# Conv, causal attention and a mixture of experts on one core: when batch 0's last row sums and its results' gathers are issued

## The chip, the core and the metric

The kernel runs on one core of one Trainium2 chip. Its time is the device time of one execution in microseconds (us). The core has five engines that each work through their own list of instructions in order: PE (matrix products), DVE and ACT (elementwise work), POOL (elementwise work and indirect DMAs), and SP (which here only issues DMAs). The engines wait for each other through semaphores. PE reads its weights and its moving operand from SBUF and writes to PSUM; an output tile in PSUM is one "bank".

## The reference

Two images of 256 channels and 56 x 56 points go through a non-local convolution block, then, as 3136 tokens of 256 values each, through causal attention with four heads and through a mixture of eight experts of which each token uses its two best:

```python
# x: (2, 256, 56, 56)
x = conv_block(x)                      # groups of 1x1 convolutions, f = theta^T phi / n, y = f g, output 1x1, relu(. + x)
t = x.reshape(2, 256, 3136).transpose(0, 2, 1)
t = t + attention(layernorm(t))        # 4 heads of 64, causal, softmax, output projection
h = layernorm(t)
probs = softmax(h @ gate_w + gate_b)   # 8 experts
top2_vals, top2_idx = top_k(probs, 2)
for e in range(8):                     # only tokens that chose e have a weight
    y_e = gelu(h @ W1[e] + b1[e]) @ W2[e] + b2[e]     # 256 -> 512 -> 256
    t = t + weight_e[:, None] * y_e
out = t.transpose(0, 2, 1).reshape(2, 256, 56, 56)
```

## The kernel before, in words

**Attention** (`attend`, about L709 to L983). The queries are cut into rows of 448 (seven rows, `i`), the heads into two pairs (`hp`). For each row and pair the kernel goes over blocks of 128 keys: PE makes scores (L806), ACT their exponentials (L810), DVE adds these up in a tile `acc` (L829), and three steps later PE multiplies them with the values (L857) into a tile `yp`. There is one buffer of `yp` (two banks), so the first product of the next row and pair waits until ACT has copied the last one out (L867). POOL then adds the two halves of that copy (L868). The sums over the exponentials are made on PE by `sum_rows` (L878, four products with ones), copied by ACT (`store_sums`, L889) and sent to DRAM and back by SP, since the inverse is needed four steps later. If `sum_rows` was already issued for a row and pair, `acc` has been read, and L867 reuses it as its target (`both`); if not, `both` is a new buffer: from the pool of the scores' exponentials (tag "st", five buffers), or from that of `acc` at the very end. For rows `i > 0` the sums are issued before the values of the last blocks, for row 0 behind them. The visit called `final` belongs to the last row and pair of batch 1; its sums come behind everything.

**Experts** (`experts`, L1578 on). The (token, expert) pairs are sorted into blocks of 128 slots. A block's pass is one turn of the loop in `experts`: `hidden` (L1673, sixteen products), the transposes of the next input (L1650), `outputs` (L1692, eight products), with ACT's gelu (L1682) between, DVE's copy of a part of the next weights (L1661) and DVE's addition of the bias into a tile `ys` (L1702, two of them), of which there are three buffers. The first 42 blocks hold batch 0 only, the next 15 both batches, the rest batch 1. Blocks below 57 (`MIXED`) are stored as they are to the DRAM tensor `y_slots` by SP (L1707). Blocks from 42 on are scattered by POOL, with an indirect DMA, to the rows of `y_tokens` (L1713), where each token of batch 1 finds its two results. The last three blocks (99 and up) are kept in SBUF and placed by products with one-hot matrices (`place`, L1784) whose column numbers stand in three tiles `hots`.

**Bringing the results home** (`finish`, L1859 on). When block 56 has been put out, `written()` (L2277) opens the buffers for this and puts two generators into the queue, batch 1's ahead of batch 0's. Every turn, `meanwhile()` (L2286) sets the counters `gathered` and `stored` to 0 and asks the queue for four pieces. For batch 0 a piece is one gather by POOL (`fetch`, L1878: an indirect DMA of 128 rows of `y_slots`; 50 in all, four for each pair of token chunks), or a pair of adds by DVE (`add`, L1913: `res_f` and `y_f`), or a `store`: four transposes on PE (L1927, names `yo_f<-ident,res_f`), a copy by ACT into `ot` (L1932, two buffers for both batches together) and a store by SP (L1933). The condition at the head of the gather's loop sets how many gathers a turn may hold; `since` is the turn in which the generator starts. For batch 1 a piece is the load of `y_tokens` by SP (`load`, L1898), the adds (L1913, written into `y_f`) and the `store` (`yo_f<-ident,y_f`); they follow the blocks' progress and not the gathers. The last pairs of token chunks are treated by `last_rows`, `add_rows`, `place_rows` and `store_last` (L1744 to L1804). Three instructions of `number_columns` (L1854, an iota on POOL into `hots`) are issued between batch 0's gathers.

Instructions are issued on each engine in the order in which this program writes them; no scheduler moves them.

Of the kernel before, what the change touches and what calls it, by code (L numbers as in the profile page):

```python
# [10 lines left out]
F32 = mybir.dt.float32  # L11
# [17 lines left out]
def conv_attn_moe_kernel(  # L29
# [51 lines left out]
    nc = tc.nc  # L81
    P = 128
    B, C, N = x.shape
    NH = C // P
# [9 lines left out]
    NB = N // W  # L94
# [11 lines left out]
    OFF = 16 * N  # L106
# [4 lines left out]
    GB = 3  # L111
# [9 lines left out]
    LAST = max(n for n in range(NCH) if complete(n) <= DIRECT)  # L121
    REST = N - LAST * P
# [65 lines left out]
    with tc.tile_pool(name="c_w", bufs=1) as cw, tc.tile_pool(name="c_s", bufs=2) as cs, tc.tile_pool(  # L188
        name="c_big", bufs=5, space=PSUM
# [11 lines left out]
        for b in range(B):  # L201
            for col in (0, C + 1):
                nc.gpsimd.memset(xr[b][:, :, col : col + 1], 1.0)
            n = 0
# [54 lines left out]
        def channels():  # L259
# [12 lines left out]
            base=0, pattern=[[-D, G], [0, D]], channel_multiplier=1,  # L272
# [3 lines left out]
            base=D - 1, pattern=[[D, G], [0, D]], channel_multiplier=-1,  # L276
# [234 lines left out]
    def layer1(nm, general):  # L511

        with ExitStack() as whole:
# [195 lines left out]
            def attend(qT, kT, v, fst, fs, psc, py, open_batch, visit, between, clock, later, finished):  # L709

                steps = []
# [238 lines left out]
                for n in range(len(steps) + LAG):  # L950
                    copy_sums = None
                    if n in visits:
                        visit(*visits[n])
                        b, i, hp = visits[n]
                        if i == 0 and hp + 1 == NH:
                            turn_rows(b, 1)
                        if i > 0 and visits[n] != final:
                            copy_sums = sum_rows(b, hp, i)
                        aligned()
                    if n + 1 < len(steps) and n > LAG and steps[n][2] == 0 and steps[n - LAG - 1][2] == 0 and steps[n - LAG - 1][4]:  # L960
                        if steps[n][1] > 1:
                            turn_rows(*steps[n][:2])
                    if n < len(steps):
                        b, i = steps[n][:2]
                        if n == 0 or steps[n - 1][0] != b:
                            open_batch(b)
                        between(b, i, ends[b, i] - n, (steps[n][3] + 1) * P > i * W + 1, room(n))

                    late = n >= LAG and steps[n - LAG][4]
                    if n >= LAG:  # L970
                        due(clock[0])
                        clock[0] += 1
                    if n >= LAG and not late:
                        values(n - LAG)
                    if n in visits and visits[n][1] == 0:
                        copy_sums = sum_rows(b, hp, 0)
                    if copy_sums:
                        copy_sums()
                    if n < len(steps):
                        scores(n)  # L980
                    if late:
                        values(n - LAG)
# [866 lines left out]
                        ids.extend(experts_of(len(ids) // GB))  # L1849
                    between()  # L1850

            def number_columns(a):

                nc.gpsimd.iota(  # L1854
                    hots[a], pattern=[[1, REST]], base=LAST * P - OFF, channel_multiplier=0,
                    allow_small_or_imprecise_dtypes=True,
                )

            def finish(b, oy, bufs):  # L1859

                t = ts[b]
# [1 line left out]
                def fetch(n, m, k):  # L1863

                    ys = [
                        oy.tile([P, 2, C], F32, tag=f"y{b}{c}", bufs=bufs, name=f"y{c}_{nm}{b}_{n}")
                        for c in range(2)
                    ]
                    res = oy.tile([P, 2, C], F32, tag="res", bufs=bufs + 1, name=f"res_{nm}_{n}")
                    rows = res[:k, :m]  # L1870
                    nc.sync.dma_start(out=rows, in_=rest_d[:k, n : n + m])
                    ahead.append((n, m, k, ys, rows))
                    for c, y in enumerate(ys):
                        for a in range(m):
                            while gathered[0] == (1 if turn[0] < since + 4 else 2 - (turn[0] % 4 == 0)) or turn[0] < since + 2:
                                yield False
                            gathered[0] += 1
                            nc.gpsimd.indirect_dma_start(  # L1878
                                out=y[:k, a],
                                out_offset=None,  # L1880
                                in_=y_slots,
                                in_offset=bass.IndirectOffsetOnAxis(
                                    ap=idxs[b][:k, c, n + a : n + a + 1], axis=0
                                ),
                                bounds_check=MIXED * P - 1,
                                oob_is_err=False,
                            )
                            yield True
# [48 lines left out]

                ahead, added, since = deque(), None, turn[0]
                parts = deque(pairs())
                steps = deque(range(GB))  # L1940
                if b:
                    parts = deque([(0, 1, P), *pairs(1, LAST)])
                while b == 0 and (parts or ahead):
                    if parts:
                        yield from fetch(*parts.popleft())
                        if len(parts) % 2 == 0 and steps:
                            number_columns(steps.popleft())
                    if len(ahead) == bufs or not parts:
                        now = ahead.popleft()
                        yield from add(*now)  # L1950
                        if added:
                            while stored[0]:
                                yield False
                            store(*added)
                            yield True
                        added = now
# [296 lines left out]
            with ExitStack() as moe:  # L2253
                mw = pool(moe, "mw", bufs=1)
                ex = pool(moe, "ex", bufs=2)
                es = pool(moe, "es", bufs=3)
                ps6 = pool(moe, "ps6", space=PSUM)
                for k in range(len(w2s), KH):
                    t = mw.tile([P, E, C], F32, name=f"w2s{k}_{nm}")
                    w2s.append(t)  # L2260
                    for e in range(0, E, 2):
                        nc.sync.dma_start(
                            out=t[:, e : e + 2],
                            in_=w2[e : e + 2, k * P : (k + 1) * P].rearrange("e p d -> p e d"),
                        )
                for _ in load_w2(True):
                    pass
                while len(early_rows) < EARLY * GB:
                    pull(every=True)

                def need(b):
                    while not sent[b]:
                        pull(every=True)
                    while not ranked[b]:
                        next(side[0])

                def written():  # L2277
                    spread_rows.close()
                    oy = pool(moe, "oy", bufs=2, side="right")
                    last_pool.append(oy)  # L2280
                    hot = pool(moe, "hot", bufs=1, side="right")
                    hots.extend(hot.tile([P, REST], F32, name=f"hot{a}_{nm}") for a in range(GB))
                    queue.append(finish(0, oy, 2))
                    queue.appendleft(finish(1, oy, 3))

                def meanwhile():  # L2286
                    gathered[0] = stored[0] = 0
                    turn[0] += 1
                    if placed[1] and not sent[1]:
                        pull(1 + turn[0] % 2, every=True)  # L2290
                    else:
                        pull(
                            4 if worked[0] >= MIXED or projected[1] and not sent[1] or not chosen[0] else 2, every=True
                        )
                    if side and next(side[0], None) is None:
                        side.popleft()

                def amid():
                    if placed[1] and not sent[1]:
                        pull(every=True)  # L2300

                def settle():
                    while queue:
                        gathered[0] = stored[0] = 0
                        pull(every=True)

                def decide():
                    if not general:
                        assert judged
                        verdict.append(count(1))  # L2310

                with tc.manual_schedule(engines={PE, DVE, POOL, SP, ACT}):
                    experts(
                        first[0], w2s, b2s, ex, es, ps6,
                        meanwhile, amid, need, written, settle, decide,
                    )
# [172 lines left out]
```

## Time and profile before

| | us |
|---|---|
| median of three runs (lowest, highest) | 1267.23 (1265.88, 1269.42) |
| the profiled execution | 1266.76 |
| its span, first to last instruction | 1264.9 |
| L1673, the experts' first product: busy | 196.2 |
| L1713, 57 scatters on POOL: busy | 59.6 |
| L1661, 102 copies of weights on DVE: busy | 71.4 |
| DVE `res_f` L1913 waiting for a gather (2 times) | 1.1 |
| span's end after the last product's start (1257.41) | 7.5 |

The profile is of one execution. A row of its groups gives line, engine, operation, output and inputs by the program's names, shapes and count, then the busy time in us, the mean duration of one in ns, and the engine's idle time just before such instructions with what ended most of it. "issue" means that the engine waited for nothing that the profile shows. In the list of waits a line gives who waited for whom, the total in us, the number of times and the longest. A timeline row gives start and length in us, with the idle time before it in brackets. Ends of matmuls are modelled, so that neighbouring rows overlap a little.

The granted PE clock is full in all 40 slices of the span (mean 0.999). The chain of work that ended last runs over PE for nearly its whole length, with L1673 (14%), L1692 (13%), L806 (7%) and L857 (7%) the largest.

### The profile page before, as it was taken

How to read it: one execution, taken by the hardware profiler on the slowest of the kernel's cores; microseconds unless marked ns; L12 is line 12 of the kernel's file. 1: busy time of each engine (PE TensorE's matmuls, PEld its weight loads, DVE VectorE, ACT ScalarE, POOL GpSimd, SP SyncE). 2: the span in 40 equal slices, each digit the busy share in tenths (PEclk: the TensorE clock that was granted, in tenths of full speed). 3: DMA queues.
4: the chain of work that ended last, by engine and by line, in shares of the span. 5: the costliest groups of instructions: out<-in, count | busy, mean ns of one | idle time of the engine just before them, and what ended most of it. 6: DMA issues, size and time to landing. Idle time of an engine off the chain costs nothing.

```text
span 1264.9 us, 28755 instructions
## 1 busy us (share of the span) xinstructions
PE 1242.6 (98%) x10881; PEld 848.1 (67%) x10881; DVE 772.8 (61%) x1687; ACT 610.7 (48%) x1237; POOL 348.9 (28%) x318
## 2 busy tenths in 40 slices
PE   8999999999999999999999999999999999999997
PEld 8876655555454545655555444479889999988886
DVE  2582567666676574566677888785744443455563
ACT  0255555565656555465555656563334333343432
POOL 1103231110021103211111656000266012666650
PEclk9999999999999999999999999999999999999999
DMA  9996101000000000100000223641344433556653
GB/s 316 352 344 194 28 24 38 25 15 26 14 17 16 1 26 21 35 23 13 9 16 25 72 67 115 218 119 60 101 143 148 121 106 92 161 180 207 208 169 116
DMA packets 119875, 125.93 MB, mean 100 GB/s; under 512 B 28375, under 2 KB 109640, under 8 KB 119730
## 3 DMA queue, kind: packets, MB, share of 16 engines
q1 hardware_dynamic: 109074, 97.45, 25.3%
q0 software_dynamic: 9840, 25.67, 6.1%
q8 instruction: 90, 1.47, 0.5%
q10 hardware_dynamic: 816, 0.88, 0.2%
q14 instruction: 55, 0.45, 0.1%
HBM read 62.06 MB, written 61.05 MB: 97 GB/s over the span
## 4 chain that ended last, share of the span: by engine, by line
PE 47%; DVE 2%; issue 1%; ACT 0%; DVEq 0%
PE ht_f L1673 14%; PE yp_f L1692 13%; PE sc_f L806 7%; PE yp_f L857 7%; PE tp_f L1650 2%; PE pp_f L682 1%; PE yo_f L1927 1%; DVE y_f L1913 1%; PE qk_f L613 1%; PE v_f L628 0%; PE tail_f L1784 0%; DVE acc_f L829 0%; PE sp_f L878 0%; ACT st_f L810 0%; PE bp_f L1405 0%
## 5 line engine op out<-in xcount | busy, mean ns | idle before, releaser
L810 ACT ACTIVATE st_f<-sc_f 128x896 f32<-128x896 f32 (+5 forms) x400 | 331.2, 839 | 189.7 <-PE sc_f L806 164.4
L829 DVE TENSOR_TENSOR acc_f<-acc_f,st_f 128x896 f32<-128x896 f32 (+6 forms) x344 | 343.9, 1000 | 105.3 <-ACT st_f L810 93.2
L806 PE MATMUL sc_f<-qT_f,kT_f 64*64 64x448 f32 (+5 forms) x3136 | 345.3, 499 | 0.5 <-issue 0.3
L857 PE MATMUL yp_f<-st_f,v_f 64*64 64x448 f32 (+4 forms) x2896 | 323.5, 511 | 1.1 <-ACT acc_f L867 0.6
L806 PEld LDWEIGHTS sc_f<-qT_f,kT_f 64*64 64x64 f32 x3136 | 140.7, 133 | 133.6 <-issue 108.1
L1682 ACT ACTIVATE g_f<-ht_f,b1b 128x128 f32<-128x128 f32 x408 | 116.5, 371 | 226.1 <-PE ht_f L1673 111.4
L857 PEld LDWEIGHTS yp_f<-st_f,v_f 64*64 64x64 f32 x2896 | 122.5, 133 | 129.1 <-issue 105.0
L1673 PE MATMUL ht_f<-xT_f,w_f 128*128 128x128 f32 x1600 | 196.2, 275 | 4.0 <-issue 3.9
L1673 PEld LDWEIGHTS ht_f<-xT_f,w_f 128*128 128x128 f32 x1600 | 192.8, 192 | 8.8 <-issue 4.7
L1537 POOL DMA_INDIRECT x_slots<-xr_f,idx x100 | 113.6, 1136 | 148.4 <-DVE xr_f L1535 75.0
L868 POOL TENSOR_TENSOR qT_f<-acc_f 128x448 f32<-128x448 f32 x22 | 25.5, 1161 | 380.3 <-ACT acc_f L867 380.2
L1661 DVE COPY w_f<-w1s_f 128x1024 f32 x102 | 71.4, 701 | 86.0 <-PE ht_f L1673 38.6
L584 POOL TENSOR_SCALAR xn_f<-t 128x256 f32<-128x256 f32 (+1 forms) x50 | 80.3, 1613 | 130.0 <-DVE t L185 44.1
L1713 POOL DMA_INDIRECT y_tokens<-ys_f,to_f x57 | 59.6, 1046 | 126.4 <-DVE ys_f L1702 100.8
L1702 DVE TENSOR_TENSOR ys_f<-yp_f,kT_f 128x128 f32<-128x128 f32 x102 | 29.4, 289 | 96.6 <-PE yp_f L1692 63.6
L613 PE MATMUL qk_f<-px_f,wat 128*128 128x512 f32 (+2 forms) x224 | 87.2, 541 | 0.6 <-ACT px_f L605 0.6
L613 PEld LDWEIGHTS qk_f<-px_f,wat 128*128 128x128 f32 x224 | 40.6, 190 | 39.7 <-issue 33.7
L1692 PE MATMUL yp_f<-w2s_f,g_f 128*128 x204 | 60.9, 379 | 0.5 <-issue 0.5
L1692 PE MATMUL yp_f<-px_f,g_f 128*128 x204 | 61.1, 381 | 0.0
L1878 POOL DMA_INDIRECT y_f<-y_slots,idx x50 | 56.6, 1132 | 15.3 <-issue 15.3
L1692 PE MATMUL yp_f<-kT_f,g_f 128*128 x204 | 60.7, 379 | 0.0
L1692 PE MATMUL yp_f<-v_f,g_f 128*128 x204 | 60.7, 379 | 0.0
(299 smaller groups left out, 1308.0 us busy)
## 6 DMA issues: line engine op xcount, KB each, us to landing
x_slots<-fill SPq DMA_DIRECT2D x1, 8190.0 KB
xb_f<-x_slots SPq DMA_DIRECT2D x60, 130.0 KB
x_slots<-fill SPq DMA_DIRECT2D x1, 7296.0 KB
y_slots<-ys_f SPq DMA_DIRECT2D x57, 128.0 KB
kept<-t SPq DMA_DIRECT2D x2, 3200.0 KB
x<-in_x_dram SPq DMA_DIRECT2D x14, 448.0 KB
rb_f<-inverses SPq DMA_DIRECT2D x56, 112.0 KB
y_f<-y_tokens SPq DMA_DIRECT2D x23, 256.0 KB
```

The source lines that it names most:

```text
L584: nc.gpsimd.tensor_scalar(xn[:k, a], ts[b][:k, n + a, :C], ts[b][:k, n + a, MEAN : MEAN + 1], ts[b][:k, n + a, RSTD : RSTD + 1], ALU.subtr ...
L613: nc.tensor.matmul(ps[:, :w], wat[:, c, d0 : d0 + P], px[:, s % 2, c, :w], start=(c == 0), stop=(c == NH - 1),)
L806: nc.tensor.matmul(to, left, right, start=True, stop=True)
L810: nc.scalar.activation(st[rows, :, c0:], ps[rows, :, c0:W], AF.Exp, scale=SCALE)
L829: nc.vector.tensor_tensor(acc[rows, :, c0:], acc[rows, :, c0:], st[rows, :, c0:], ALU.add)
L857: nc.tensor.matmul(to, left, right, start=first, stop=end)
L1537: s = nc.gpsimd.indirect_dma_start(out=xds[b], out_offset=bass.IndirectOffsetOnAxis(ap=idxs[b][:kk, k, n : n + 1], axis=0), in_=xr[:kk], i ...
L1661: nc.vector.tensor_copy(w, w1s[:, :, bass.ds(e, 1), :].rearrange("p c e h -> p c (e h)"))
L1673: nc.tensor.matmul(ht[:, k, :], w[:, c, k * P : (k + 1) * P], xT[:, c, :], start=(c == 0), stop=(c == NH - 1),)
L1682: nc.scalar.activation(g[:, k, :], ht[:, k, :], AF.Gelu, bias=b1bs[b][:, k, i : i + 1])
L1692: nc.tensor.matmul(yp[:, :C], g[:, k, :], w2s[k][:, bass.ds(e, 1), :].rearrange("p e d -> p (e d)"), start=(k == 0), stop=(k == KH - 1),)
L1713: s = nc.gpsimd.indirect_dma_start(out=y_tokens, out_offset=bass.IndirectOffsetOnAxis(ap=to[:, n % GB : n % GB + 1], axis=0), in_=ys, in_o ...
```

## The change

Three edits.

1. In `attend`, the visit of batch 0's last row (`i == NB - 1`), second pair, is treated as those of row 0 are: its `sum_rows` is issued behind `values`. The same visit of batch 1 stays `final`.
2. The three iotas go from the gathers' loop into `written()`, one behind the other.
3. The gathers' loop waits under another condition. Before: none for two turns, then one a turn up to the fourth turn, then two, or one in every fourth turn. After: one a turn for eight turns, the first in the turn in which the generator starts, then one and two by turns.

```diff
-                        if i > 0 and visits[n] != final:
+                        short = i == 0 or (i, hp) == (NB - 1, NH - 1)
+                        if i >= 0 and not short:
                             copy_sums = sum_rows(b, hp, i)
                         aligned()
...
                     if n >= LAG and not late:
                         values(n - LAG)
-                    if n in visits and visits[n][1] == 0:
-                        copy_sums = sum_rows(b, hp, 0)
+                    if n in visits and short and visits[n] != final:
+                        b, i, hp = visits[n]
+                        copy_sums = sum_rows(b, hp, i)
                     if copy_sums:
                         copy_sums()
...
-            def number_columns(a):
-
-                nc.gpsimd.iota(
-                    hots[a], pattern=[[1, REST]], base=LAST * P - OFF, channel_multiplier=0,
-                    allow_small_or_imprecise_dtypes=True,
-                )
-
             def finish(b, oy, bufs):
...
-                            while gathered[0] == (1 if turn[0] < since + 4 else 2 - (turn[0] % 4 == 0)) or turn[0] < since + 2:
+                            while gathered[0] == (1 if turn[0] < since + 8 else 1 + turn[0] % 2):
                                 yield False
...
-                steps = deque(range(GB))
...
-                        if len(parts) % 2 == 0 and steps:
-                            number_columns(steps.popleft())
...
-                    hots.extend(hot.tile([P, REST], F32, name=f"hot{a}_{nm}") for a in range(GB))
+                    for a in range(GB):
+                        hots.append(hot.tile([P, REST], F32, name=f"hot{a}_{nm}"))
+                        nc.gpsimd.iota(
+                            hots[a], pattern=[[1, REST]], base=LAST * P - OFF, channel_multiplier=0,
+                            allow_small_or_imprecise_dtypes=True,
+                        )
```

The numbers of instructions on each engine are the same before and after; only their order differs. In that order the gathers of batch 0 stand like this against the scatters of blocks (S56 is block 56's scatter, G a gather, I an iota):

```
before: S57 S58G S59G S60GGI S61GG S62GG S63G S64GG S65GI S66GG S67G S68G S69GG S70GG S71I S72GG ... S89GG S90G S91G S92
after:  S56IIIG S57G ... S63G S64GG S65G S66G S67G S68GG S69G S70GG S71G S72G S73G S74GG ... S92GG S93G S94 S95GG S96
```

Batch 1's transposes stand where they stood. Batch 0's stand later: those of the pair at chunk 0 two turns later, at 12 three, at 20 and 22 four, and at 24 behind batch 1's at 17, in the last rows' part. On SP the stores of batch 0's pairs 20 and 22 thereby come behind the two loads (L1898) of batch 1's pair 19, which wait for the buffer of pair 17.

## The prediction

> **What bounds the kernel.** I read the engine table, then the waits over the whole run, then the timeline of the places the diff touches.
>
> ```profile
> PE 1242.6 (98%) x10881; PEld 848.1 (67%) x10881; DVE 772.8 (61%) x1687; ACT 610.7 (48%) x1237; POOL 348.9 (28%) x318
> ...
> L1702 DVE TENSOR_TENSOR ys_f<-yp_f,kT_f 128x128 f32<-128x128 f32 x102 | 29.4, 289 | 96.6 <-PE yp_f L1692 63.6
> ...
> L1878 POOL DMA_INDIRECT y_f<-y_slots,idx x50 | 56.6, 1132 | 15.3 <-issue 15.3
> ```
>
> PE is busy for 98% of the span of 1264.9 us: only what removes idle PE time, or shortens the start or the tail, can pay. No arithmetic is removed, so the prize is at most the idle PE time that the moved work causes. POOL is 28% busy, but its 50 gathers lie between 1082 and 1221, and there this average means nothing.
>
> **The gathers.** One expert block ("turn") is 16 matmuls of L1673, two of L1650 and eight of L1692. In the stretch before the gathers (990 to 1091) turns start exactly 3.73 us apart; a transpose of L1927 adds 0.11. From the end of one block's L1692 row at 1091.15 to another's at 1225.60 there are 32 turns and 75 transposes: 32 x 3.7325 + 75 x 0.11 = 127.7 us, but 134.45 passed. **6.8 us are lost here**, all in turns in which batch 1's transposes wait for DVE's adds (the profile's modelled waits give 4.2 us in 7 cases to L1927 <- DVE y_f L1913). The worst turn, PE first, then DVE, then POOL (start, length; idle in brackets):
>
> ```profile
> 1113.95 0.59 PE L1692 MATMUL yp_f<-w2s_f,g_f 128*128 x2
> 1115.70 0.33 PE L1927 MATMUL yo_f<-ident,y_f 128*128 128x128 f32 x1 [1.16 <-DVE y_f L1913]
> 1116.62 0.55 PE L1927 MATMUL yo_f<-ident,y_f 128*128 128x128 f32 x3 [0.59 <-DVE y_f L1913]
> ```
>
> ```profile
> 1109.92 0.85 DVE L1661 COPY w_f<-w1s_f 128x1024 f32 x1 [0.45 <-PE tp_f L1650]
> 1113.66 0.29 DVE L1702 TENSOR_TENSOR ys_f<-yp_f,kT_f 128x128 f32<-128x128 f32 x1 [2.89 <-PE tp_f L1650]
> 1113.87 0.28 DVE L1702 TENSOR_TENSOR ys_f<-yp_f,v_f 128x128 f32<-128x128 f32 x1
> 1114.64 0.48 DVE L1913 SCALAR_TENSOR_TENSOR y_f<-y_f,t 128x256 f32<-128x256 f32 x1 [0.50 <-issue]
> ```
>
> ```profile
> 1106.27 1.21 POOL L1713 DMA_INDIRECT y_tokens<-ys_f,to_f  x1 [2.16 <-DVE ys_f L1702]
> 1107.78 1.19 POOL L1878 DMA_INDIRECT y_f<-y_slots,idx  x1 [0.30 <-issue]
> 1109.28 1.00 POOL L1878 DMA_INDIRECT y_f<-y_slots,idx  x1 [0.30 <-issue]
> 1110.58 1.07 POOL L1713 DMA_INDIRECT y_tokens<-ys_f,to_f  x1 [0.30 <-issue]
> 1111.96 1.02 POOL L1878 DMA_INDIRECT y_f<-y_slots,idx  x1 [0.31 <-issue]
> ```
>
> The reader is to see that POOL runs without a rest, and that L1702, which before 1091 starts 0.20 us after its matmul has ended, starts here at 1113.66 for a matmul that ended at 1110.65: 3.0 late. The adds of L1913 stand behind it on DVE, and PE stops for them. A POOL DMA is about 1.0 us with 0.30 after it: two gathers and a scatter fill 3.9 us, more than a turn; one gather and a scatter fill 2.6. The late starts sort themselves by that: after two turns with two gathers each they are 1.7 to 3.0 us, after a single such turn mostly 0.2 to 0.7. Why a full POOL delays DVE, the trace does not say; that part is inference from a pattern.
>
> The old pace is one gather, then 2, 2, 2, 1 by turns, beginning two turns after block 56; the new one is one a turn for eight turns, beginning at once, then 1, 2, 1, 2. In the order of instructions no two turns in a row have two gathers any more; the first gather comes two turns earlier, the last some four turns later (behind the scatter of block 96 at the latest, in place of 92). So POOL needs 6.5 us in each two turns of 7.46. I expect the late starts to fall under about 1 us, which a batch 1 transpose bears (gaps appear from 1 to 2 us). Bounds: all 6.8 back, or nothing. **I take 5.4**, four fifths, since a turn with two gathers still meets some of batch 1's adds, and three times two adds of batch 0 (0.48 each) now follow batch 1's four in the same turn.
>
> Here a rule speaks against the change. The Trainium skill, "SBUF — State Buffer", in the box 'The "DVE blocks DMA" trap (SWDGE)', says that an fp32 SBUF-to-SBUF copy on DVE locks GpSimd out of the shared port while it writes a DMA's descriptors. Such a copy (L1661, 0.69 us) stands in every turn. Were that what fills POOL, spacing would not help, each gather would meet a copy anyway, and this part would bring nothing (sum: +0.85 us). The rows: gathers take 1.00 to 1.54 us, so a copy can cost one of them about 0.5, not the 2 to 3 us of the late starts; and two gathers a turn fill the turn even at 1.0. I go by the rows; the rule is part of why I don't take all 6.8.
>
> **The iotas.** Three of 0.52 us move from between gathers to before the first: 1.56 us on POOL after block 56's results. POOL was free there from 1074.4 to 1077.2, and no scatter waits. Cost 0. With the cover gone the first gather would be 1.5 us later, which a first add many turns on does not feel. The first gather waits for the last store to y_slots (issued by SP at 1073.2); at about 1076.3 that has landed if it takes 3 us, else POOL stalls for a fraction of a turn: cost 0 to 0.3 on POOL, taken 0 on PE.
>
> **The row sums.** In batch 0's last row, second pair, PE runs L878 (0.52 us), then the last values (L857), then waits 0.59 us at 475.69 for ACT to empty the one bank of yp:
>
> ```profile
> PE yp_f L857 <- ACT acc_f L867: 0.6, 1, 0.6
> ```
>
> With the sums behind the values ACT's copy starts 0.52 earlier, and the sums cover PE meanwhile: 0.5 to 0.59 us of gap go. Late next are PE's own matmuls. New: `both` takes one of the "st" buffers until POOL's add (L868, 1.13 us) is done, as every first row already does. If scores had to wait for that buffer, up to 0.5 would return. ACT's copy of the sums (0.35) and the loads behind it come up to 0.5 later, needed four steps on. **I take -0.55**; ends -0.6 and 0.
>
> **The tail, where something is added.** Batch 0's last stores slip: its transposes at 20 and 22 come three and four turns later, at 24 four (now directly behind batch 1's at 17). PE does the same number. But SP is a queue: the stores of 20 and 22 now stand behind the two loads of y19, which wait for a buffer that batch 1's transpose at 17 frees (they issue at 1250.75 and 1251.17). So store 20 issues at about 1251.65. `ot` has two buffers, in the order 20, 22, 17, 24, 19: the copy for 17 (L1932, 0.59) waits for store 20 to land, and the copy for 19, which ends the chain, waits for store 17 to land. With a landing time L after the issue, copy 19 can start at 1251.65 + 2L + 0.62 = 1252.27 + 2L; now it starts at 1258.05. The point from which this costs is L = 2.9 us. No row gives L for such a store in the middle. Nearest below: the second load of y19, issued 1251.17, used at 1254.31, so 3.1. Above: the last store, issued 1258.66, seen landed by SP at 1263.17, 4.5 with the last rows' stores ahead of it in the rings. Cost 0.4 to 3.3 us; nearer the lower, since store 17 flies alone but store 20 does not: L = 3.6, **+1.4 us**.
>
> **The sum.** -5.4 - 0.55 + 1.4 = -4.55 us. The profiled execution took 1266.76 us, of which 1264.9 is span: 1262.2, span 1260.35. The median of the three runs shown is 1267.23, 0.47 above that execution: **1262.7 us**. What this kernel's measurement can tell from no change is about 0.3%, 3.8 us; the forecast lies just beyond.
>
> **Rivals.**
> *The late starts stay.* They follow the number of gathers or the copy on DVE, not the density; the gaps only move to other turns. For it: 50 gathers before and after, more turns with gathers in them, and batch 1's transpose at 15 now close to their end. Against: turns with one gather show 0.2. Taking back 1.4 of the 6.8: 1267.23 - 0.55 - 1.4 + 1.4 = 1266.7.
>
> *The tail decides.* The two landings in series at the upper L = 4.5 cost 3.3. If the gathers' part gives nothing, the kernel is slower from L = 3.2 on (2L - 5.8 > 0.55); at 4.5 it is 1267.23 - 0.55 + 3.3 = 1270.0; if that part gives its 5.4, L would have to pass 5.9. For it: the queue order and buffers are fixed by the program. Against: no store's landing of such length is shown away from the crowded end.
>
> *The pacing does not take hold,* since pulls are shared with batch 1's work and gathers bunch anyway. The order of instructions shows them spread, so this has little: 1267 to 1268.
>
> **Chances.** Forecast 0.5 (own range 1260.0 to 1264.5: tail 0.4 to 3.3, gathers 4 to 6.8); late starts stay 0.27 (1264 to 1268.5); tail decides 0.17 (1267.5 to 1272); no hold 0.06. Leaving out a tenth at each side: 1259.5 to 1270.3. Faster by over 0.3% means under 1263.4: nearly all of the forecast's case, 0.47. Slower means over 1271: part of the tail's case and what I have not seen, 0.14. Within: 0.39.
>
> **What would show it.** Right: L1702's rows from 1080 to 1240 start under 1 us after their matmul, the wait L1927 <- DVE y_f L1913 falls from 4.2 to about 1, the wait of L857 for ACT at 475 is gone. Tail: ACT idles ahead of the copies for 17 and 19, and the time from the last L1927 to the last copy grows from 0.02 by about 1.4. Wrong: late starts of 2 us after turns with one gather; DVE rows waiting for gathers (now 1.1 us in two cases) or PE waiting for batch 0's adds, which would mean that the later results have become late themselves.

## The result, and the profile after

The changed kernel takes 1261.39 us (median of 7 runs, 1260.51 to 1263.36), the kernel before, beside it, 1267.23 (7 runs, 1265.34 to 1270.32): a ratio of 0.9958, 95% interval 0.9944 to 0.9972. That is 5.8 us, against the 4.6 forecast. The profiled execution has a span of 1259.3 us, 5.6 less than before.

The page's rows that answer to those shown of before:

```profile
PE 1241.6 (99%) x10881; PEld 849.1 (67%) x10881; DVE 775.7 (62%) x1687; ACT 611.0 (49%) x1237; POOL 348.8 (28%) x318
...
L1704 DVE TENSOR_TENSOR ys_f<-yp_f,kT_f 128x128 f32<-128x128 f32 x102 | 29.5, 289 | 89.3 <-PE yp_f L1694 66.3
...
L1873 POOL DMA_INDIRECT y_f<-y_slots,idx x50 | 56.1, 1123 | 17.1 <-issue 17.1
```

The same work, spread differently. The list of waits has lost L857 <- ACT acc_f (0.6 before), and of the 4.2 us for batch 1's adds this is left:

```profile
PE yo_f L1922 <- DVE y_f L1908: 0.9, 2, 0.4
```

To see where the time went, I set the two profiles beside each other matmul by matmul: the k-th product of a kind in one against the k-th in the other. The difference in start, after minus before:

```
where (time in before)          after - before, us
behind the start, 100 to 460        -0.98
after the row sums, 480             -1.50     the edit in attention: -0.52
760 to 880                          -2.30
routing done, 990                   -0.20     all of it given back
gathers begin, 1085                 -0.20
behind the gathers' stretch, 1235   -6.90     of which 1.3 are batch 0's transposes, moved behind it
last product, 1258                  -5.56
end of the span                     -5.6
```

So the whole gain lies between 1085 and 1258. The sum that gave 6.8 us of lost PE time before gives 1.5 us now. Batch 1's adds tell why. Seven groups of four lie in this stretch (the first group, of two, is left out); how late L1702 (L1704 after) starts just ahead of each:

```
group           2      3      4      5      6      7      8
before, us    3.01   0.20   2.65   2.53   2.43   2.13   2.41
after, us     0.89   1.06   0.20   1.87   1.08   0.20   1.46
```

Up to 1.08 PE does not wait; from 1.46 on it does. Over the whole stretch the late starts fell from a mean of 1.09 us to 0.78 and from at most 3.01 to 2.09, but starts more than 1 us late are hardly rarer: 15 of 34 turns before, 15 of 40 after.

The tail, in ACT's timeline of the changed kernel:

```profile
1248.99 0.94 ACT L1927 COPY ot_f<-yo_f 128x512 f32<-128x512 f32 x2 [6.77 <-DMA out_dram<-ot_f]
1251.30 0.53 ACT L1804 COPY hot_f<-tail_f 128x448 f32<-128x448 f32 x1 [1.38 <-PE tail_f L1786]
1251.87 0.40 ACTq L1805 DMA_DIRECT2D out_dram<-hot_f  x1
1253.49 0.58 ACT L1927 COPY ot_f<-yo_f 128x512 f32<-128x512 f32 x1 [1.66 <-DMA out_dram<-ot_f]
1254.11 0.38 ACTq L1928 DMA_DIRECT2D out_dram<-ot_f  x1
```

The first row is the copy for chunk 17 (with that for 24), which had to wait for store 20; the fourth is the copy for 19, which waits for store 17. Both waits stand where the prediction put them. Against PE's last product the last copy is 1.0 us later than before.

### The profile page after: what moved, and what is told of

Same layout as the page of the kernel before. It is cut to its first block, busy times and chain, and to the rows that moved or that the text cites. A ratio compares the mean times of both kernels' runs of the same rounds, so it can differ in the third digit from the quotient of the medians.

```text
span 1259.3 us, 28754 instructions
## 1 busy us (share of the span) xinstructions
PE 1241.6 (99%) x10881; PEld 849.1 (67%) x10881; DVE 775.7 (62%) x1687; ACT 611.0 (49%) x1237; POOL 348.8 (28%) x318
## 4 chain that ended last, share of the span: by engine, by line
PE 47%; DVE 1%; issue 1%; DMA 1%; ACT 0%; DVEq 0%; SPq 0%; ACTq 0%
PE ht_f L1675 14%; PE yp_f L1694 14%; PE yp_f L857 7%; PE sc_f L806 7%; PE tp_f L1652 2%; PE pp_f L682 1%; PE yo_f L1922 1%; PE qk_f L613 1%; DMA out_dram<-ot_f 1%; PE v_f L628 0%; DVE y_f L1908 0%; DVE acc_f L829 0%; PE sp_f L878 0%; PE bp_f L1407 0%; ACT st_f L810 0%
## 5 line engine op out<-in xcount | busy, mean ns | idle before, releaser
L857 PE MATMUL yp_f<-st_f,v_f 64*64 64x448 f32 (+4 forms) x2896 | 323.6, 511 | 0.5 <-DVE st_f L813 0.3
L857 PEld LDWEIGHTS yp_f<-st_f,v_f 64*64 64x64 f32 x2896 | 122.5, 133 | 128.2 <-issue 104.8
L1675 PE MATMUL ht_f<-xT_f,w_f 128*128 128x128 f32 x1600 | 197.4, 276 | 3.2 <-issue 3.2
L1675 PEld LDWEIGHTS ht_f<-xT_f,w_f 128*128 128x128 f32 x1600 | 193.4, 192 | 9.4 <-issue 5.0
L1704 DVE TENSOR_TENSOR ys_f<-yp_f,kT_f 128x128 f32<-128x128 f32 x102 | 29.5, 289 | 89.3 <-PE yp_f L1694 66.3
L1694 PE MATMUL yp_f<-w2s_f,g_f 128*128 x204 | 61.3, 381 | 0.2 <-issue 0.2
L1694 PE MATMUL yp_f<-kT_f,g_f 128*128 x204 | 61.1, 381 | 0.0
L1694 PE MATMUL yp_f<-v_f,g_f 128*128 x204 | 61.1, 381 | 0.0
L1694 PE MATMUL yp_f<-px_f,g_f 128*128 x204 | 61.1, 381 | 0.0
```

The lines of the kernel that those rows point to most:

```text
L857: nc.tensor.matmul(to, left, right, start=first, stop=end)
L1675: nc.tensor.matmul(ht[:, k, :], w[:, c, k * P : (k + 1) * P], xT[:, c, :], start=(c == 0), stop=(c == NH - 1),)
L1694: nc.tensor.matmul(yp[:, :C], g[:, k, :], w2s[k][:, bass.ds(e, 1), :].rearrange("p e d -> p (e d)"), start=(k == 0), stop=(k == KH - 1),)
```

## The experiments

The experiments ran on four chips (numbered 11, 1, 6 and 12), each with the kernel before beside it, and **on all four the kernel before takes 1250.4 to 1250.9 us, not 1267**. The chip of the result's own runs is not on record, nor is whether the chip or the hour made the difference. So what follows compares each kernel with the kernel before on its own chip; "the first place" is where and when the result was measured. Nothing but the two kernels of the result was measured there.

### The kernel before once more, and the three edits one at a time (chip 11)

> The kernel before, profiled once more, to see how far one execution differs from another. Theory (the change's gain lies in the gathers' stretch): PE's pace from 990 on is that of the first profile, with about 6.8 us lost between 1091 and 1226, while single differences of 0.5 to 2 us in the stretches before 990 (the load at the start, the routing between 885 and 986) come and go from execution to execution. Rival (those differences belong to the change): this profile agrees with the first one within 0.3 us everywhere before 990.

The program is instruction for instruction the same, and its span is 1248.2 us, 16.7 less. Matmul by matmul: 0.9 us at the start, 2.1 between 690 and 800 and 5.9 between 900 and 986 (in both stretches POOL scatters `x_slots`), nothing from 986 to 1090, 6.9 in the gathers' stretch, and 1.0 behind the last product. The theory fails where it seemed surest: between the gathers nothing is lost, and L1702 is 0.20 us late in all 34 turns with gathers. Here is a stretch with two gathers a turn, POOL, then DVE, then PE:

```profile
1096.85 1.02 POOL L1878 DMA_INDIRECT y_f<-y_slots,idx  x1 [0.30 <-issue]
1098.17 1.00 POOL L1878 DMA_INDIRECT y_f<-y_slots,idx  x1 [0.30 <-issue]
1099.48 1.02 POOL L1713 DMA_INDIRECT y_tokens<-ys_f,to_f  x1 [0.31 <-DVE res_f L1913]
1100.80 1.43 POOL L1878 DMA_INDIRECT y_f<-y_slots,idx  x1 [0.31 <-issue]
1102.24 0.52 POOL L1854 IOTA hot_f<- 128x448 f32 x1
1102.93 1.02 POOL L1713 DMA_INDIRECT y_tokens<-ys_f,to_f  x1 [0.17 <-issue]
```

```profile
1101.86 0.29 DVE L1702 TENSOR_TENSOR ys_f<-yp_f,kT_f 128x128 f32<-128x128 f32 x1 [0.52 <-PE yp_f L1692]
1102.06 0.28 DVE L1702 TENSOR_TENSOR ys_f<-yp_f,v_f 128x128 f32<-128x128 f32 x1
1102.84 0.55 DVE L1913 SCALAR_TENSOR_TENSOR y_f<-y_f,t 128x256 f32<-128x256 f32 x1 [0.50 <-issue]
```

```profile
1104.95 0.59 PE L1692 MATMUL yp_f<-w2s_f,g_f 128*128 x2
1105.38 0.60 PE L1927 MATMUL yo_f<-ident,y_f 128*128 128x128 f32 x4
```

This is the very turn that cost 2.2 us in the first place. POOL is as full, with the same iota between, and yet L1702 follows its matmul (end 1101.65) by 0.2 us, the adds end at 1104.83, and PE runs into batch 1's four transposes at 1105.38 without a stop. A full POOL is not enough to make the late starts.

> Only the row sums of batch 0's last row, second pair, go behind the values. Theory: the gap of 0.59 us at 475 goes, and PE runs 0.5 us ahead from there; but the routing stage between 885 and 986 swallows it, because it waits for a chain that is not PE's, so that from 990 on PE stands where it stood before: total 0 to -0.5 us (1266.7 to 1267.2). Rival: the 0.5 us reaches the end, and part of the change's 5.6 us is due to it: -0.5 us or more.

```diff
-                        if i > 0 and visits[n] != final:
+                        short = i == 0 or (i, hp) == (NB - 1, NH - 1)
+                        if i >= 0 and not short:
                             copy_sums = sum_rows(b, hp, i)
...
-                    if n in visits and visits[n][1] == 0:
-                        copy_sums = sum_rows(b, hp, 0)
+                    if n in visits and short and visits[n] != final:
+                        b, i, hp = visits[n]
+                        copy_sums = sum_rows(b, hp, i)
```

1250.91 us against 1250.74: ratio 1.0002 (0.9993 to 1.0010). PE gains 0.52 us at 475, loses 0.19 of it near 780, and the rest at the routing, where this line appears that the kernel before does not have:

```profile
PE rank_f L1291 <- DVE both_f L1243: 0.5, 1, 0.5
```

PE arrives 0.5 us early for a product whose operand a chain on DVE makes, and waits. The changed kernel shows the same line in both places. The theory holds: the edit pays 0.5 us and nothing of it reaches the end.

> Only the condition of the gathers' loop is changed; iotas and row sums stay. Theory: nearly all of the change's gain, -5 to -6 us (1261 to 1262): between 1091 and 1226 PE loses 1.5 us in place of 6.8, and the copy of chunk 19 waits about 1 us for a store. Rival (the iotas between the gathers matter): -3 us or less, with late starts of 2 to 3 us where an iota stands between two gathers.

```diff
-while gathered[0] == (1 if turn[0] < since + 4 else 2 - (turn[0] % 4 == 0)) or turn[0] < since + 2:
+while gathered[0] == (1 if turn[0] < since + 8 else 1 + turn[0] % 2):
```

1251.11 us: ratio 1.0003 (0.9995 to 1.0011). Neither theory is met: where the kernel before has no late starts, there is nothing to gain. What remains is the tail: the copy for 17 waits 6.9 us for a store and that for 19 another 2.0. In its profile the span is 1.8 us longer than in the one just shown; 0.7 of that stand from the start of the kernel on, 1.1 come behind PE's last product.

> Only the three iotas go to the front of the gathers. Theory: nothing that can be measured, 0 +- 0.5 us, as 1.56 us of 57 us of POOL's work go from the crowded stretch: the late starts of L1702 stay at 1.7 to 3.0 us. Rival (the iotas fill POOL just where it overflows): -1 to -3 us, with the worst turn at 1110 gone.

The edit is the change's second part alone (the iotas in `written()`). 1250.58 us, ratio 1.0000 (0.9992 to 1.0008): no effect, as expected, though without the late starts it can't be told what they would do in the first place.

### The changed kernel elsewhere, and its tail (chip 1)

> The changed kernel itself once more, beside the kernel before on the same chip. In the four runs before this one the kernel before took 1250.7 us and L1702 was never late between the gathers, where the first profile had 1.7 to 3.0 us. Theory A (the late starts are a condition of where it runs, and the change only treats them): where the kernel before shows no late starts (about 1250), the change is worth -0.5 to +1 us; where it shows them (about 1267), -5 to -6 us. Theory B (the change is worth 5 us anywhere, by its three edits together): -5 us here too.

1251.39 against 1250.72 us: ratio 1.0005 (0.9997 to 1.0013). Theory A: the change is worth 5.8 us in one place and nothing in another (it is 0.7 us slower, within the noise). ACT's last copies, chunk 17 with 24 and then 19:

```profile
1239.79 0.94 ACT L1927 COPY ot_f<-yo_f 128x512 f32<-128x512 f32 x2 [6.96 <-DMA out_dram<-ot_f]
...
1244.57 0.59 ACT L1927 COPY ot_f<-yo_f 128x512 f32<-128x512 f32 x1 [2.13 <-DMA out_dram<-hot_f]
```

> The changed kernel with three buffers for the tile that the copies of L1927 fill, in place of two. Theory (two landings in series hold up the last copy by 1.0 us in the profile after, 2.0 with the pacing alone): the copy of chunk 17 waits no longer for the store of 20, nor 19's for that of 17; ACT's waits for a store fall from 8.4 us to 0; the end comes 0.5 to 2 us earlier than in the changed kernel. Rival (the wait costs nothing, since the last store then has the DMA engines to itself): same time within 0.3 us.

```diff
-                    ot = oy.tile([P, NH, 2 * P], F32, tag="ot", bufs=2, name=f"ot_{nm}{b}_{n}")
+                    ot = oy.tile([P, NH, 2 * P], F32, tag="ot", bufs=3, name=f"ot_{nm}{b}_{n}")
```

The copies for 17 and 19 no longer wait for a store (that for 24 still does, 3.6 us), and copy 19 starts 1.44 us earlier:

```profile
1235.42 0.59 ACT L1927 COPY ot_f<-yo_f 128x512 f32<-128x512 f32 x1 [2.57 <-issue]
...
1243.13 0.59 ACT L1927 COPY ot_f<-yo_f 128x512 f32<-128x512 f32 x1 [0.66 <-PE yo_f L1922]
```

but the kernel takes 1251.32 us, the same as with two buffers: in time the rival is right. In its profile the last store was issued at 1243.75 and its last packets moved at 1248.07, 4.3 us later; with two buffers it was issued at 1245.19 and done at 1247.53, 2.3 us later. The other last stores had moved by 1245.6 in both. What the copy waits less, its store takes longer. Why is not shown: its last packets moved 2.5 us behind those of the other stores.

### More gathers a turn (chip 1)

> The kernel before with three gathers in every turn instead of one or two, and room in the queue's turn for them (12 pieces in place of 4). Three gathers and a scatter fill 5.2 us of POOL, more than a turn's 3.73, for all 17 turns. Theory A (a full POOL delays what DVE and ACT see of PE, anywhere): late starts of L1702 of 1 to 3 us in most of these turns also where the kernel before shows none, PE loses 5 us or more, time +3 to +8 us. Theory B (a full POOL alone does nothing; the late starts are a condition of where it runs): where the kernel before takes about 1250, L1702 keeps its 0.20 us save where its own buffer is not free; time within 1 us of before, or lower, as the stores come earlier.

```diff
-while gathered[0] == (1 if turn[0] < since + 4 else 2 - (turn[0] % 4 == 0)) or turn[0] < since + 2:
+while gathered[0] == 3 or turn[0] < since + 2:
...
-                            4 if worked[0] >= MIXED or projected[1] and not sent[1] or not chosen[0] else 2, every=True
+                            12 if worked[0] >= MIXED or projected[1] and not sent[1] or not chosen[0] else 2, every=True
```

1287.7 us, ratio 1.0294 (1.0276 to 1.0311), far beyond either theory, and in its time not a clean test. The 12 pieces also act on an earlier stage: 13 us are lost before the first gather. And in the gathers' stretch the adds now come right behind their gathers, so that DVE, in order, stops for the landing:

```profile
DVE res_f L1913 <- DMA y_f<-y_slots,idx: 35.7, 21, 5.0
```

(1.1 us in two cases in the first profile). It shows what the queue's small piece count is worth: the distance between a gather and its add hides the landing. DVE's late starts here, up to 6.8 us and in 10 of the 17 turns, can't be told from such waits.

ACT can be read, though, since its gelus (L1682) don't stand behind those waits. In the first place it saw PE late as DVE did. I count the gelus ahead of which ACT stood idle, and how late each begins after the last product of L1673 ahead of it. In the kernel before 13 of 27 in the gathers' stretch are more than 0.4 us late, at most 3.8, and 13 of 19 between 900 and 990, but none of 25 between these stretches, where the most is 0.20. In the changed kernel it was 13 of 29 and 12 of 18. Here POOL issues for 92 us without a rest:

```profile
1140.05 1.00 POOL L1878 DMA_INDIRECT y_f<-y_slots,idx  x1 [0.30 <-issue]
1141.36 0.99 POOL L1878 DMA_INDIRECT y_f<-y_slots,idx  x1 [0.30 <-issue]
1142.66 1.02 POOL L1713 DMA_INDIRECT y_tokens<-ys_f,to_f  x1 [0.30 <-issue]
1143.99 1.42 POOL L1878 DMA_INDIRECT y_f<-y_slots,idx  x1 [0.31 <-issue]
1145.71 1.00 POOL L1878 DMA_INDIRECT y_f<-y_slots,idx  x1 [0.30 <-issue]
```

and all 16 such gelus are at most 0.35 us late. So on this chip a POOL as dense as in the worst turn, and for 92 us on end, does not make ACT see PE late.

### Stores from another queue; POOL busy without DMAs (chip 6)

> The changed kernel with the stores of batch 0's pairs 18, 20, 22 and 24 issued from ACT's queue, right behind their copies, so that they don't stand behind the loads of y19 on SP. Theory (the tail's cost is SP's order; more buffers did not help because the stores themselves were still late): ACT's waits for a store (7.0 and 2.1 us in the changed kernel) go, the stores of 20 and 22 land 5 us earlier, the last 3 us have the DMA engines to themselves; 0.5 to 1.5 us less than the changed kernel, so at about 1250 no more than the kernel before. Rival (ACT, in order, is held by 0.4 us for each issue and delays gelus): no gain or a loss of up to 1 us.

```diff
-                            store(*added)
+                            store(*added, nc.scalar if added[0] >= LAST - 5 else nc.sync)
                             yield True
...
-                    store(*added)
+                    store(*added, nc.scalar)
                     return
```

ACT no longer waits for a store, and the last product (1242.08 us) and the last store's last packet (1245.45) stand where they stand in the kernel before (1242.01 and 1245.43, in the profile of chip 11). Yet it takes 1252.53 us against 1250.44: ratio 1.0017 (1.0009 to 1.0025), 2.1 us slower than the kernel before, where the changed kernel was 0.7 slower on chip 1. The expectation fails, and so does its rival, behind the work: SP, in its closing waits, stands still from 1246.13 to 1248.14, when the data has long moved. Why is open; in the one profile there is one more 8 KB fetch of instructions in the tail than in that profile of the kernel before, the last at 1248.78.

> Only the pacing, once more, on the chance of a place where the kernel before takes about 1267. There: the theory that the pacing carries the change's gain expects -5 to -6 us; the rival (iotas or row sums carry it) at most -3. Where the kernel before takes about 1250: +0.4 us as in the first run.

1251.55 us against 1250.44: ratio 1.0008 (1.0001 to 1.0014). Again there are no late starts to remove, and here the small loss, 1.1 us, is just clear of the noise.

> The kernel before with each of the 50 gathers replaced by four iotas on POOL into the same tile (batch 0's tokens are given numbers in place of their experts' results): POOL is as busy, but issues no DMA. Where the kernel before takes about 1267: if a busy POOL makes the late starts, they stay at 1.7 to 3.0 us and PE loses 6 us; if it is the gathers' DMAs, they are gone and PE loses nothing. Where it takes about 1250 there are none in either case, and the run shows only that.

```diff
-                            nc.gpsimd.indirect_dma_start(
-                                out=y[:k, a],
-                                out_offset=None,
-                                in_=y_slots,
...
+                            for _ in range(4):
+                                nc.gpsimd.iota(
+                                    y[:k, a], pattern=[[1, C]], base=0, channel_multiplier=0,
+                                    allow_small_or_imprecise_dtypes=True,
+                                )
```

```profile
1095.39 0.99 POOL L1713 DMA_INDIRECT y_tokens<-ys_f,to_f  x1 [0.43 <-DVE ys_f L1702]
1096.39 2.01 POOL L1879 IOTA y_f<- 128x256 f32 x4
1098.83 1.08 POOL L1713 DMA_INDIRECT y_tokens<-ys_f,to_f  x1 [0.43 <-DVE ys_f L1702]
1099.92 3.61 POOL L1879 IOTA y_f<- 128x256 f32 x8
1103.96 1.22 POOL L1713 DMA_INDIRECT y_tokens<-ys_f,to_f  x1 [0.43 <-DVE y_f L1908]
```

This kernel leaves the gathers out, so that batch 0's output is wrong, and has a single run, 1252.12 us. POOL is fuller than with gathers (four iotas take 2.0 us), scatters slip by up to 4 us, and L1702 is 0.20 to 0.38 late in 32 of 34 turns; in one of the others its row names the wait, a scatter that still holds its buffer. So where there are no late starts, neither a POOL full of iotas nor, in the run with three gathers a turn, a POOL full of DMAs makes them. The half of the question that needs the first place was not answered.

### The start alone, and the rule about DVE's copies (chip 12)

> The kernel before with its old densities (one gather, then 2, 2, 2, 1), but beginning two turns earlier; iotas and row sums stay. Where the kernel before takes about 1267: if spacing the gathers is what pays, this brings nothing (within 1 us); if their start is, -4 us or more. Where it takes about 1250: the stores of batch 0 come two turns earlier than before, so the tail stays as it was and the time is that of the kernel before within 0.5 us, against +0.4 to +1.1 us with the new pacing.

```diff
-while gathered[0] == (1 if turn[0] < since + 4 else 2 - (turn[0] % 4 == 0)) or turn[0] < since + 2:
+while gathered[0] == (1 if turn[0] < since + 2 else 2 - (turn[0] % 4 == 0)):
```

1250.4 against 1250.6 us: ratio 0.9998 (0.9989 to 1.0007). The tail stays as it was; no copy waits for a store. Of the new paces tried it is the only one that shows no cost there, and it is not measurably better than the kernel before.

> The kernel before with the copy of the weights (L1661, fp32 from SBUF to SBUF, 0.69 us on DVE) put on ACT for blocks 57 to 98, so that no DVE copy meets a gather. Where the kernel before takes about 1267: if the copy's hold on a port shared with POOL makes the late starts, they go and the time falls by 5 us or more; if not, they stay. Where it takes about 1250 there is nothing to gain: gathers take 1.00 to 1.10 us each in place of up to 1.5, ACT has about 1.1 us more a turn and stays under 3.73, time within 1 us of before, or a few us more if ACT's order delays the gelus.

```diff
-                    engines=(PE, DVE),
+                    engines=(PE, DVE, ACT),
...
-                    nc.vector.tensor_copy(
+                    copy = nc.scalar.copy if MIXED <= n < DIRECT else nc.vector.tensor_copy
+                    copy(
                         w, w1s[:, :, bass.ds(e, 1), :].rearrange("p c e h -> p c (e h)")
```

1250.68 us, ratio 0.9998 (0.9989 to 1.0007). The gathers' rows, first with the copy on DVE (chip 11), then with it on ACT:

```profile
L1878 POOL DMA_INDIRECT y_f<-y_slots,idx x50 | 55.7, 1115 | 15.3 <-issue 15.0 <-PE tp_f L1650 0.3
```

```profile
L1879 POOL DMA_INDIRECT y_f<-y_slots,idx x50 | 51.6, 1032 | 15.3 <-issue 14.7 <-PE tp_f L1650 0.3 <-DMA xb_f<-x_slots 0.3
```

Ten of the 50 gathers took over 1.3 us (at most 1.48) beside the copies on DVE; none does without (at most 1.21). The median stays 1.02. The rule of the Trainium skill that the prediction weighed, "SBUF — State Buffer", 'The "DVE blocks DMA" trap (SWDGE)', is seen here, in the size that the prediction read from the rows: up to half a microsecond for a gather that meets a copy, 4 us of POOL in all, and nothing of the time. Whether it has a part in the first place's late starts was not tested there.

## Why the prediction was right, and how far

**The gathers: right in size, in its place, and in part by luck.** -5.4 was taken, and 6.8 - 1.5 = 5.3 is what the aligned profiles give. The mechanism holds as far as this: shorter delays reach batch 1's adds, and up to 1.08 us PE does not feel them. But three statements of that step are wrong.

First, the late starts were to fall under about 1 us; they fell to at most 2.1, and as many turns as before have more than 1. Even the prediction's own sign of being wrong, 2 us after turns with one gather each, is there, at block 60:

```profile
1087.22 2.15 PE L1675 MATMUL ht_f<-xT_f,w_f 128*128 128x128 f32 x16
1088.66 0.69 DVE L1663 COPY w_f<-w1s_f 128x1024 f32 x1 [3.45 <-PE yp_f L1694]
1088.66 1.14 ACT L1684 ACTIVATE g_f<-ht_f,b1b 128x128 f32<-128x128 f32 x4 [5.28 <-PE yp_f L1694]
1089.27 0.28 DVE L1704 TENSOR_TENSOR ys_f<-yp_f,kT_f 128x128 f32<-128x128 f32 x1
```

(The product of L1694 had ended when L1675 starts, at 1087.22.)

Second, what paid is which turns are hit, and this the forecast did not work out. Before, the late starts of over 2 us come every four turns from block 74 on (74, 78, 82, 86, 90), and so do batch 1's adds: six of the seven groups meet such a start. After, the long ones come every six turns (72 and 73, 78 and 79, 84 and 85, 90 and 91), and two of the seven groups meet one. That the size came out right is to this extent luck.

Third, "a full POOL delays DVE" is not enough of a cause. In the first place, late starts came only where POOL issued DMAs densely (0.20 at most between 1000 and 1070), so density belongs to it; on the chips as dense a stream gave none, and one without a rest did not make ACT's gelus late. (With the new pacing three starts are 0.8 us late there, at blocks 67, 79 and 91, where the adds of both batches fall into one turn, as the forecast had said.) There is a second condition, which the first trace could not show because it was present throughout. The prediction flagged the cause as an inference from a pattern, and that is what failed when tested. The rival "the late starts stay" is what the counts look like; its time was wrong because it did not ask which turns they hit.

**The row sums: right locally, off at the end.** -0.55 was taken and -0.52 appears at 475. "Late next are PE's own matmuls" was the wrong half: next is the routing's chain on DVE, 410 us further on, and PE waits 0.46 us for it. The term is 0.

**The iotas:** 0 in the forecast; 0 alone on chip 11. But in the first place POOL stood idle for 2.1 us between the iotas and the first gather, where at most 0.3 was forecast, then issued seven DMAs without a rest; the late start at block 60 comes right behind these, and PE lost 0.2 us there.

**The tail: the copies right, the end not.** Two landings in series at L = 3.6 us each was the step; the trace has 3.3 from the issue of store 20 (1245.65) to the copy it frees (1248.99), and 3.9 from store 17 (1249.60) to copy 19 (1253.49). The last copy came 1.0 us later against PE, in place of 1.4. The step that failed is the next one, that the end moves with this copy. From the start of PE's last row to the end of the span, in every profile but that of three gathers a turn:

```
                                        us
old pacing   the first place            7.5
             six profiles on the chips  6.5 to 6.7
new pacing   the first place            7.5
             three on the chips         7.7 to 7.9
             three buffers              7.8     copies 17 and 19 don't wait
             stores from ACT's queue    8.5     no copy waits
```

In the first place the net is 0, because there the kernel before already took 6.3 us from its last store's issue to the end, and 5.3 to 5.4 in the six profiles elsewhere. On the chips the new pacing costs about 1.1 us here, near the 1.4 (in the medians 0.4 to 1.1). But where the copies no longer wait, the loss stays. So what costs is not their wait, or not it alone; what it is stays open.

Sum: -5.3 + 0 + 0 = -5.3 between the gathers' start and the end, with -0.2 from before it, against -5.6 measured. The forecast's -4.55 was short by the tail (+1.4) and long by the row sums (-0.55).

Some small slips of the working change nothing: 0.4 of the 6.8 us were lost in turns without a wait for batch 1's adds; POOL was free until 1078.69 and not 1077.2; the upper L = 4.5 costs 3.2 us, not 3.3; and with the costs named the range reaches 1266.0, not 1264.5.

What stays open: what differs between the first place and the four chips, what in the new pacing makes the tail longer, and whether in the first place the pacing alone carries the gain. The pacing without the iotas' move was never run there, so that the split between these two rests on the iotas' small share of POOL (1.6 us) alone.

## What to carry to other kernels

Before a wait is explained by what stands beside it in one trace, profile the same program a second time elsewhere: here 16.7 of 1265 us, and all of what the change removed, belonged to where or when it ran. A change that spaces out one engine's work can then be worth 0.4% in one place and nothing in another, so the gain should be quoted with its place. For a delay in an in-order engine, ask which of its consumers has the least slack: halving the delay ahead of batch 1's adds (2.2 to 1.0 us on average) removed four fifths of the loss, because the loss begins only past that slack. And where two patterns repeat, compare their periods: a delay that comes every four turns meets each piece of work that does, one that comes every six meets fewer.

## What the runs showed of the hardware

- One program on five occasions: 1267 us in one place, 1250.4 to 1250.9 on four chips. Of the excess, 14.9 us sit in the three stretches where POOL issues indirect DMAs closely (2.1 and 5.9 us while `x_slots` is scattered, 6.9 between the gathers). The DMAs themselves were no slower there: 4 KB packets of POOL's queue between 1085 and 1200 took 0.208 us on average in both.
- In the first place the delay was in what the other engines saw of PE: at 1109.92 ACT's first gelu began in the same instant as DVE's copy L1661 in the prediction's rows, and both were released by PE.

```profile
1109.92 1.14 ACT L1682 ACTIVATE g_f<-ht_f,b1b 128x128 f32<-128x128 f32 x4 [1.83 <-PE tp_f L1650]
```

- A full POOL alone does not do this: on chip 1, with POOL at work for 92 us without a rest, the gelus were at most 0.35 us late.
- Moving the last copy 1.44 us earlier left the time as it was (1251.32 against 1251.39 us): its store, issued that much earlier, took 4.3 us in place of 2.3.
